# Expert rows transposed two blocks ahead, the gate's deviation by Newton steps on VectorE, and sorting by single spaced operations

## The chip, the cores and the metric

The kernel runs on one NeuronCore of a Trainium2 chip. Its engines work side by side, each through its own instructions in order: TensorE (PE, with its weight loads PEld), VectorE (DVE), ScalarE (ACT), GpSimd (POOL) and SyncE (SP), which here only issues DMAs. The metric is the device time of one execution in microseconds. The kernel before took 1323.85 us, the median of three runs (1323.38 to 1324.76).

## The reference

Two images of 256 channels and 56 x 56 points (N = 3136 tokens of C = 256) go through a linear non-local block, causal attention with 4 heads, and a mixture of 8 experts of which each token uses two. All is float32.

```python
x = _L0_conv_ref(x, ...)                       # non-local block, batch norm, + x, relu
t = _to_tokens(x)
t = t + _L1_attn_ref(_ln_t(t), W_attn, W_proj) # 4 heads, causal softmax
t = t + _L1_ffn_ref(_ln_t(t), gate_w, gate_b, W1, b1, W2, b2)
...
def _ln_t(v, eps=1e-5):
    m = jnp.mean(v, axis=-1, keepdims=True)
    s = jnp.var(v, axis=-1, keepdims=True)
    return (v - m) / jnp.sqrt(s + eps)
...
logits = xf @ gate_w + gate_b
probs = jax.nn.softmax(logits, axis=-1)
top2_vals, top2_idx = jax.lax.top_k(probs, 2)
# for each of the 8 experts, with its weight we per token:
h = jax.nn.gelu(xf @ w1 + bb1, approximate=False)
acc = acc + we[:, None] * (h @ w2 + bb2)
```

## The kernel before

A token tile is 128 tokens; an image has 25 (NCH), the last of 64 tokens. The kernel computes an expert's result only for the tokens that chose it: it sorts the two choices of every token into slots of DRAM tables `x_slots`, in blocks of 128 rows with one expert each, and works through 105 blocks (NBLK). The first 42 (FULL0) are filled by image 0 alone; the next 15 (up to MIXED = 57) may hold rows of both images; the rest belong to image 1.

**Stages.** The non-local block fills the first 96 us. Attention follows, image 0 up to about 495 us and image 1 up to 885 us. The experts run from 885 us to 1300 us, and a short tail writes the last outputs.

**Attention** (`attend`). Queries go in 7 blocks of 448; for each block and each pair of heads `hp` the key tiles are walked. A step computes scores on PE (L649), their Exp on ACT (L657), the causal mask on diagonal tiles (L659) and the running sum of the exponentials on DVE (L671), and three steps later (LAG) the values product on PE (L689). The result of a block lies in one PSUM buffer (`py`, bufs=1); ACT and DVE empty it at L699 and L700, and the next block's L689 waits for that. The division by the row sums makes a journey through DRAM: matmul with ones (L716), copy (L721), DMAs, reciprocal on DVE (L736), DMAs, product (L748). Each step of it is queued some steps after the one before.

**The order** is written by hand. Everything else is written as generators that yield between pieces; a `yield True` counts as a piece of work, a `yield False` says that nothing can be done now. In attention, `between` runs ahead of every score tile: in odd turns it pulls two pieces from `queue`, in even ones it issues steps of the projection to q, k and v (`project_qkv`). `pull` takes the next piece from the first generator in the queue that has one. The order in which pieces are issued is the order on each engine, and every engine keeps it.

For each image the queue has `tokens(b)`: `project_out` (attention's output projection for a tile, L598; sum and statistics on DVE, L603, L159, L160), then `dispatch(b)`, and for image 0 the loading of `w1s` (eight DMAs of 512 KB on SP), whose room is that of image 0's rows. So `dispatch(0)` and `project_out(1)` share the pulls during image 1's attention; `dispatch(1)` runs in the experts.

**`dispatch`** computes the gate and the sort: the deviation of each token (`inverse_deviation`: Sqrt on ACT, L166, reciprocal on DVE, L167), the gate's logits from sums that were made before (L955, L958), softmax (L961 to L967, with an Exp on ACT at L963), two maxima with their experts (L979 to L986), the ranks by matmuls with triangular and full ones (L1001, L1003), the slots (L1005 to L1077), the experts of the blocks (`first_blocks`, `last_blocks`, `one_hot`), and the scatter: for each tile the normalised rows (L1209, two buffers for image 0) and two indirect DMAs on POOL (L1217). Nearly all are small operations on DVE, of 128 x 200 or less. They are issued several at a time between yields (`small_piece`: three yields for image 0, one for image 1).

**`experts`**. Iteration n issues, in this order: the fetch of a group of three blocks from `x_slots` (`fetch`, six blocks ahead), the combination of a group's rows (`load`, two ahead; image 1's groups compute their places, L1281 to L1286, and mixed groups add rows, L1289), `hidden(n)` (16 matmuls at L1335, four Gelu on ACT at L1344), `inputs(n + 1)` (two transposes on PE at L1312, one copy to `xT` on ACT at L1316), `weights(n + 2)` (the expert's w1 copied by DVE, L1323), `outputs(n - 3)` (eight matmuls L1354, the bias on DVE, L1364, and the stores), and `between`: two or three pulls and one step of image 1's `last_blocks`. PSUM has two buffers each for transposes, hidden and output; `xT` has three, `w` two. The fetch of the first image 1 group comes at n = 36 and needs image 1's scatter.

Of the kernel before, what the change touches and what calls it, by code (L numbers as in the profile page):

```python
# [11 lines left out]
I32 = mybir.dt.int32  # L12
# [15 lines left out]
def conv_attn_moe_kernel(  # L28
# [133 lines left out]
    def inverse_deviation(b, n, m):  # L162
        r = ts[b][:, n : n + m, RSTD]

        d = ts[b][:, n : n + m, SLOT]
        nc.scalar.activation(d, r, AF.Sqrt, bias=eps5)  # L166
        nc.vector.reciprocal(r, d)  # L167
# [271 lines left out]
    def layer1(nm, general):  # L439

        with ExitStack() as whole:
# [147 lines left out]
            def project_out(b, qT, done):  # L589

                for first, m, k in pairs():
                    while done() < (first + m - 1) * P + k:
                        yield False
                    for n in range(first, first + m):
                        o = n * P
                        ps = bank(f"pp_{b}_{n}")
                        for c in range(NH):
                            nc.tensor.matmul(  # L598
                                ps[:k, : C + E], qT[:, c, o : o + k], wpr[:, c, :],
                                start=(c == 0), stop=(c == NH - 1),  # L600
                            )
                        t = ts[b][:k, n, : C + E]
                        nc.vector.tensor_tensor(t, t, ps[:k, : C + E], ALU.add)  # L603
                        stats(b, n, 1, k, bg, f"o{nm}{b}")
                        if b == 0:
                            nc.sync.dma_start(out=rest_d[:k, n], in_=t[:, :C])
                        yield True

                    for _ in range(2 if b == 0 else 0):
                        yield True  # L610
# [324 lines left out]
            def dispatch(b):  # L935
# [3 lines left out]
                inverse_deviation(b, 0, NCH)  # L939
                yield True  # L940

                def small_piece():

                    for _ in range(1 if b else 3):
                        yield True

                def small(name, last=E, dt=F32):
                    return g1.tile([P, NCH, last], dt, tag=name, name=f"{name}_{nm}{b}")
# [5 lines left out]
                red = small("red", 1)  # L954
                nc.vector.tensor_tensor(  # L955
                    pr, t[:, :, C : C + E], wide(t[:, :, RSTD : RSTD + 1]), ALU.mult
                )
                nc.vector.tensor_tensor(  # L958
                    pr, pr, gb.unsqueeze(1).to_broadcast([P, NCH, E]), ALU.add
                )  # L960
                nc.vector.tensor_reduce(red, pr, AX.X, ALU.max)  # L961
                nc.vector.tensor_tensor(pr, pr, wide(red), ALU.subtract)
                nc.scalar.activation(pr, pr, AF.Exp)  # L963
                yield from small_piece()
                nc.vector.tensor_reduce(red, pr, AX.X, ALU.add)
                nc.vector.reciprocal(red, red)
                nc.vector.tensor_tensor(pr, pr, wide(red), ALU.mult)  # L967
                yield from small_piece()


# [5 lines left out]
                for k in range(2):  # L976
                    top = wts[b][:, :, k : k + 1]
                    one = small(f"one{k}")
                    nc.vector.tensor_reduce(top, src, AX.X, ALU.max)  # L979
                    nc.vector.tensor_tensor(at, src, wide(top), ALU.is_equal)  # L980
                    nc.vector.tensor_tensor(at, at, ids, ALU.mult)
                    yield from small_piece()
                    nc.vector.tensor_reduce(red, at, AX.X, ALU.max)
                    nc.vector.tensor_tensor(one, at, wide(red), ALU.is_equal)
                    if k == 0:
                        nc.vector.scalar_tensor_tensor(left, one, -2.0, pr, ALU.mult, ALU.add)  # L986
                        src = left
                    picks.append(one)
                    yield from small_piece()
                both = small("both")  # L990
                nc.vector.tensor_tensor(both, picks[0], picks[1], ALU.add)
                if tail < P:
                    nc.vector.memset(both[tail:, NCH - 1], 0.0)
                flat = both.rearrange("p t e -> p (t e)")
                yield from small_piece()

                if b:
                    yield True
# [8 lines left out]
                )  # L1007
                tot = g1.tile([P, E, NCH], F32, tag="tot", name=f"tot_{nm}{b}")
                nc.vector.tensor_copy(tot, total[:, : NCH * E].rearrange("p (t e) -> p e t", e=E))
                yield from small_piece()  # L1010
# [22 lines left out]
                )  # L1033

                first = few("first")
                nc.vector.tensor_tensor(first, ends[:, :, NCH - 1], cnt, ALU.subtract)
                nc.vector.tensor_tensor(ends, ends, tot, ALU.subtract)
                slot = g1.tile([P, NCH, E], F32, tag="both", name=f"slot_{nm}{b}")
                nc.vector.tensor_tensor(slot, ranks, ends.rearrange("p e t -> p t e"), ALU.add)
                yield from small_piece()  # L1040
# [26 lines left out]
                nc.vector.tensor_tensor(part, slot, spread(lim), ALU.is_lt)  # L1067
                nc.vector.tensor_tensor(part, part, spread(low), ALU.mult)
                yield from small_piece()
                nc.vector.tensor_tensor(slot, slot, spread(base), ALU.add)  # L1070
                nc.vector.tensor_tensor(slot, slot, part, ALU.add)
                yield from small_piece()
                for k in range(2):
                    nc.vector.tensor_tensor(at, slot, picks[k], ALU.mult)
                    nc.vector.tensor_reduce(red, at, AX.X, ALU.add)
                    flat = red.rearrange("p t o -> p (t o)")
                    nc.vector.tensor_scalar(  # L1077
                        idxs[b][:, k, :], flat, -float(known[b][0] * P), None, ALU.add
                    )
                    if b and k == 0:  # L1080
                        nc.vector.tensor_scalar(t[:, :, SLOT], flat, 1.0, None, ALU.add)
                    yield from small_piece()

                def one_hot(eb, w):
# [5 lines left out]
                    for _ in range(1 if b else 3):  # L1090
                        yield True
# [7 lines left out]
                def first_blocks():  # L1099
# [7 lines left out]
                    )  # L1107
                    eb = g1.tile([P, MIXED], F32, tag="eb", name=f"eb_{nm}{b}")
                    nc.vector.tensor_reduce(eb, past, AX.X, ALU.add)
                    yield from small_piece()  # L1110
                    step = g1.tile([P, MIXED], F32, tag="step", name=f"step_{nm}{b}")
                    nc.vector.tensor_scalar(step, number[:, :MIXED], nfull, -float(E), ALU.is_ge, ALU.mult)
                    nc.vector.tensor_tensor(eb, eb, step, ALU.add)
                    nc.vector.tensor_scalar(step, number[:, :MIXED], nfull, 0.0, ALU.subtract, ALU.max)
# [89 lines left out]
                for n in range(NCH):  # L1204
# [11 lines left out]
                    for k in range(2):  # L1216
# [11 lines left out]
                        yield True  # L1228
# [4 lines left out]
            def experts(w1s, w2s, b2s, ex, es, ps6, between, need, written):  # L1233
# [156 lines left out]
                for n in range(-1, NBLK + LATE):  # L1390
                    while len(fetched) * GB <= min(n + 6, NBLK - 1):
                        fetched.append(fetch(len(fetched)))
                    while len(groups) * GB <= min(n + 2, NBLK - 1):
                        groups.append(load(len(groups), *fetched[len(groups)]))
# [4 lines left out]
                    if n + 1 < NBLK:  # L1399
                        xin[n + 1] = inputs(n + 1, groups[(n + 1) // GB])  # L1400
# [419 lines left out]
```

## Time and profile before

The profiled execution took 1325.2 us, 1323.5 us of it the span that the trace covers.

| what | value |
|---|---|
| median of the timed runs | 1323.85 us |
| profiled execution, its span | 1325.2 us, 1323.5 us |
| mean granted clock of PE | 0.993 |
| L671, sum of exponentials, DVE, 128x896 | 288 times, 1092 ns |
| L657, Exp of scores, ACT, 128x896 | 316 times, 918 ns |
| L598, output projection, PE, 128x264 | 192 matmuls, 403 ns |
| L1335, hidden, PE, 128x128 | 1680 matmuls, 276 ns |
| L1217, scatter, POOL | 100 times, 1153 ns |
| L963, Exp of the gate, ACT, 128x200 | 2 times, 370 ns |
| L166, Sqrt of the gate, ACT, 128x25 | 2 times, 338 ns |
| table loads of ACT | 9 times, 1283 ns |

A matmul in float32 counts as two instructions. Matmuls overlap, so their mean is longer than the time from one to the next. A line of the timeline has the start, the busy time (of all instructions that were merged into it, x16 for instance), engine, line, operation, output<-input and shape; behind it, in brackets, the time for which the engine stood idle before it, and what ended that.

### The profile page before, as it was taken

Reading aid. Unit: us, or ns where it says so; the run is one execution under the profiler, and the core shown is the slowest. Engines: PE = TensorE matmul, PEld = TensorE weight load, DVE = VectorE, ACT = ScalarE, POOL = GpSimd, SP = SyncE. Lnnn points to the kernel's source line nnn. Section 1 sums busy time; section 2 is a strip of 40 time slices with the busy share of each in tenths; the row PEclk is TensorE's granted clock in tenths of the full one; section 3 lists DMA queues with packets and bytes.
Section 4 is the critical chain, followed back from the end, with each engine's and each line's share of the span. In section 5 each row is a group of like instructions: output and inputs, shape, how many; then the busy total and the mean of one; then the engine's idle time right before and its main releaser. Section 6 shows DMA issues by size and latency. Waiting matters only on the chain.

```text
span 1323.5 us, 28216 instructions
## 1 busy us (share of the span) xinstructions
PE 1281.4 (97%) x10647; PEld 811.4 (61%) x10647; DVE 791.9 (60%) x1657; ACT 613.2 (46%) x1247; POOL 311.8 (24%) x300
## 2 busy tenths in 40 slices
PE   8999999999999999989999999998999999999994
PEld 7875444444444444434444444447999999999994
DVE  1582555757777654565958788765754344555552
ACT  0145554555555555455554456554333333344441
POOL 1113110000000111110004444000176012765541
PEclk9999999999999999999999999999999999999997
DMA  9993000000000000100001112441254333666642
GB/s 298 384 327 131 16 24 25 24 16 24 9 17 13 21 1 8 41 9 9 16 17 56 53 54 87 176 139 40 81 169 156 93 112 100 187 208 198 187 153 71
DMA packets 111048, 123.96 MB, mean 94 GB/s; under 512 B 20095, under 2 KB 100620, under 8 KB 110904
## 3 DMA queue, kind: packets, MB, share of 16 engines
q1 hardware_dynamic: 96664, 92.89, 22.8%
q0 software_dynamic: 10416, 26.00, 5.9%
q10 hardware_dynamic: 3824, 3.18, 0.8%
q8 instruction: 88, 1.44, 0.5%
q14 instruction: 56, 0.46, 0.1%
HBM read 63.04 MB, written 60.81 MB: 94 GB/s over the span
## 4 chain that ended last, share of the span: by engine, by line
PE 92%; DVE 2%; ACT 2%; DMA 1%; issue 1%; POOL 1%; SPq 0%; DVEq 0%; ACTq 0%; POOLq 0%
PE yp_f L689 21%; PE sc_f L649 19%; PE ht_f L1335 14%; PE yp_f L1354 13%; PE qk_f L535 6%; PE pp_f L598 4%; PE v_f L554 4%; PE cp L321 3%; PE gram L252 3%; PE tp_f L1312 2%; ACT st_f L657 1%; PE sp_f L716 1%; PE yo_f L1477 1%; DVE acc_f L671 1%; PE xp_f L514 1%
## 5 line engine op out<-in xcount | busy, mean ns | idle before, releaser
L657 ACT ACTIVATE st_f<-sc_f 128x896 f32<-128x896 f32 (+5 forms) x400 | 333.8, 838 | 293.8 <-PE sc_f L649 265.4
L671 DVE TENSOR_TENSOR acc_f<-acc_f,st_f 128x896 f32<-128x896 f32 (+5 forms) x372 | 366.5, 985 | 170.0 <-ACT st_f L657 163.1
L689 PE MATMUL yp_f<-st_f,v_f 64*64 64x448 f32 (+6 forms) x3184 | 342.0, 505 | 7.7 <-DVE qT_f L700 6.5
L649 PE MATMUL sc_f<-qT_f,kT_f 64*64 64x448 f32 (+6 forms) x3184 | 342.3, 501 | 0.0
L1344 ACT ACTIVATE g_f<-ht_f,b1b 128x128 f32<-128x128 f32 x420 | 120.1, 369 | 223.5 <-PE ht_f L1335 223.4
L1335 PE MATMUL ht_f<-xT_f,w_f 128*128 128x128 f32 x1680 | 205.8, 276 | 5.8 <-ACT xT_f L1316 5.8
L649 PEld LDWEIGHTS sc_f<-qT_f,kT_f 64*64 64x64 f32 x3184 | 117.6, 133 | 151.7 <-issue 137.5
L689 PEld LDWEIGHTS yp_f<-st_f,v_f 64*64 64x64 f32 x3184 | 111.7, 133 | 159.3 <-issue 132.1
L1335 PEld LDWEIGHTS ht_f<-xT_f,w_f 128*128 128x128 f32 x1680 | 201.6, 192 | 12.5 <-ACT xT_f L1316 7.7
L497 POOL TENSOR_SCALAR xn_f<-t 128x256 f32<-128x256 f32 (+1 forms) x50 | 67.1, 1351 | 549.6 <-issue 333.6
L1217 POOL DMA_INDIRECT x_slots<-xr_f,idx x100 | 115.3, 1153 | 214.9 <-DVE xr_f L1209 136.4
L1323 DVE COPY w_f<-w1s_f 128x1024 f32 x105 | 73.8, 703 | 59.8 <-PE ht_f L1335 58.5
L1371 POOL DMA_INDIRECT y_tokens<-ys_f,to_f x63 | 64.4, 1022 | 148.7 <-DVE ys_f L1364 138.9
L535 PE MATMUL qk_f<-px_f,wat 128*128 128x512 f32 (+1 forms) x224 | 92.4, 558 | 1.2 <-ACT px_f L520 1.2
L1364 DVE TENSOR_TENSOR ys_f<-yp_f,kT_f 128x128 f32<-128x128 f32 x105 | 30.5, 291 | 102.8 <-PE yp_f L1354 102.7
L659 DVE TENSOR_TENSOR st_f<-st_f,keep 128x256 f32<-128x256 f32 (+1 forms) x112 | 44.1, 394 | 66.2 <-ACT st_f L657 65.8
L535 PEld LDWEIGHTS qk_f<-px_f,wat 128*128 128x128 f32 x224 | 38.6, 190 | 54.2 <-issue 44.8
L1354 PE MATMUL yp_f<-px_f,g_f 128*128 x210 | 62.7, 381 | 0.0
L1354 PE MATMUL yp_f<-v_f,g_f 128*128 x210 | 62.5, 379 | 0.0
L1354 PE MATMUL yp_f<-w2s_f,g_f 128*128 x210 | 62.5, 379 | 0.0
L1354 PE MATMUL yp_f<-kT_f,g_f 128*128 x210 | 62.5, 379 | 0.0
L1427 POOL DMA_INDIRECT y_f<-y_slots,idx x50 | 55.4, 1108 | 16.3 <-issue 14.0
(249 smaller groups left out, 1174.4 us busy)
## 6 DMA issues: line engine op xcount, KB each, us to landing
x_slots<-fill SPq DMA_DIRECT2D x1, 8127.0 KB
xb_f<-x_slots SPq DMA_DIRECT2D x63, 129.0 KB
x_slots<-fill SPq DMA_DIRECT2D x1, 7296.0 KB
y_slots<-ys_f SPq DMA_DIRECT2D x57, 128.0 KB
kept<-t SPq DMA_DIRECT2D x2, 3200.0 KB
x<-in_x_dram SPq DMA_DIRECT2D x14, 448.0 KB
xr<-in_x_rows_dram SPq DMA_DIRECT2D x12, 512.0 KB
out_dram<-ot_f SPq DMA_DIRECT2D x24, 256.0 KB
```

The source lines that it names most:

```text
L497: nc.gpsimd.tensor_scalar(xn[:k, a], ts[b][:k, n + a, :C], ts[b][:k, n + a, MEAN : MEAN + 1], ts[b][:k, n + a, RSTD : RSTD + 1], ALU.subtr ...
L535: nc.tensor.matmul(ps[:, :w], wat[:, c, d0 : d0 + P], xT[:, c, :w], start=(c == 0), stop=(c == NH - 1),)
L649: nc.tensor.matmul(ps[h : h + HS, a, c0:W], kT[hp][rows, j * P + h : j * P + h + HS], qT[rows, hp, q0 + c0 : q0 + W], start=True, stop=True,)
L657: nc.scalar.activation(st[:k, :, c0:], ps[:k, :, c0:W], AF.Exp, scale=SCALE)
L671: nc.vector.tensor_tensor(acc[:k, :, c0:], acc[:k, :, c0:], st[:k, :, c0:], ALU.add)
L689: nc.tensor.matmul(yp[a * HS : (a + 1) * HS, h // HS, c0:W], v[hp][h : h + HS, j, a, :HS], st[h : h + HS, a, c0:], start=first, stop=bool( ...
L1217: s = nc.gpsimd.indirect_dma_start(out=xds[b], out_offset=bass.IndirectOffsetOnAxis(ap=idxs[b][:kk, k, n : n + 1], axis=0), in_=xr[:kk], i ...
L1323: nc.vector.tensor_copy(w, w1s[:, :, bass.ds(e, 1), :].rearrange("p c e h -> p c (e h)"))
L1335: nc.tensor.matmul(ht[:, k, :], w[:, c, k * P : (k + 1) * P], xT[:, c, :], start=(c == 0), stop=(c == NH - 1),)
L1344: nc.scalar.activation(g[:, k, :], ht[:, k, :], AF.Gelu, bias=b1bs[b][:, k, i : i + 1])
L1354: nc.tensor.matmul(yp[:, :C], g[:, k, :], w2s[k][:, bass.ds(e, 1), :].rearrange("p e d -> p (e d)"), start=(k == 0), stop=(k == KH - 1),)
L1371: s = nc.gpsimd.indirect_dma_start(out=y_tokens, out_offset=bass.IndirectOffsetOnAxis(ap=to[:, n % GB : n % GB + 1], axis=0), in_=ys, in_o ...
```

## The change

- **`project_out`**: image 1's two tiles of a pair are issued together and followed by two yields; before, there was a yield after each tile. Image 0 keeps its order.
- **`dispatch`, deviation**: in place of Sqrt on ACT and a reciprocal, four Newton steps for the inverse square root on DVE, with a start value from integer operations: 3 operations, then 4 x 4, all of 128 x 25. `inverse_deviation` remains for the non-local block and for the branch that isn't taken here.
- **`dispatch`, spacing**: a new generator `op` yields once or twice, in turn, after nearly every operation for image 0, and not at all for image 1; `small_piece` yields once for image 1 and not at all for image 0. The Exp of the gate gets yields ahead of it in both.
- **`dispatch`, scatter**: for image 0 one yield per tile instead of two, so that both indirect DMAs of a tile are issued together.
- **`experts`**: `inputs` runs two blocks ahead instead of one, and `load` three instead of two.

```diff
                         stats(b, n, 1, k, bg, f"o{nm}{b}")
                         if b == 0:
                             nc.sync.dma_start(out=rest_d[:k, n], in_=t[:, :C])
-                        yield True
-
-                    for _ in range(2 if b == 0 else 0):
+                            yield True
+
+                    for _ in range(2):
                         yield True
...
-                inverse_deviation(b, 0, NCH)
-                yield True
+                ops = [0]
 
                 def small_piece():
 
-                    for _ in range(1 if b else 3):
+                    if b:
+                        yield True
+
+                def op():
+
+                    ops[0] += 1
+                    for _ in range(0 if b else 1 + ops[0] % 2):
                         yield True
...
+                var = t[:, :, RSTD]
+                x, y, z = (
+                    small(k, 1).rearrange("p t o -> p (t o)") for k in ("newton_x", "newton_y", "red")
+                )
+                nc.vector.tensor_scalar(x, var, 1e-5, None, ALU.add)
+                nc.vector.tensor_scalar(
+                    y.bitcast(I32), x.bitcast(I32), 1, None, ALU.arith_shift_right
+                )
+                nc.vector.tensor_scalar(
+                    y.bitcast(I32), y.bitcast(I32), -1.0, float(0x5F3759DF), ALU.mult, ALU.add
+                )
+                yield from small_piece()
+                for i in range(4):
+                    to = var if i == 3 else y
+                    nc.vector.tensor_tensor(z, y, y, ALU.mult)
+                    nc.vector.tensor_tensor(z, z, x, ALU.mult)
+                    nc.vector.tensor_scalar(z, z, -0.5, 1.5, ALU.mult, ALU.add)
+                    nc.vector.tensor_tensor(to, y, z, ALU.mult)
+                    yield from op()
+                    yield from small_piece()
...
                 nc.vector.tensor_tensor(pr, pr, wide(red), ALU.subtract)
+                yield from op()
+                yield from small_piece()
                 nc.scalar.activation(pr, pr, AF.Exp)
                 yield from small_piece()
+                yield from op()
                 nc.vector.tensor_reduce(red, pr, AX.X, ALU.add)
+                yield from op()
...
-                        yield True
+                        if b or k:
+                            yield True
                     if b == 0:
                         yield False
...
-                    while len(groups) * GB <= min(n + 2, NBLK - 1):
+                    while len(groups) * GB <= min(n + 3, NBLK - 1):
                         groups.append(load(len(groups), *fetched[len(groups)]))
...
-                    if n + 1 < NBLK:
-                        xin[n + 1] = inputs(n + 1, groups[(n + 1) // GB])
+                    for m in (n + 1, n + 2):
+                        if m < NBLK and m > n + 1 - (n < 0):
+                            xin[m] = inputs(m, groups[m // GB])
```

Behind almost every other operation of `dispatch` stands the same `yield from op()`.

## The prediction, made before the changed kernel had run

> **What bounds the kernel now.** First the page: PE is busy 1281.4 us of a span of 1323.5 us, and it carries the chain of waits.
>
> ```profile
> PE 1281.4 (97%) x10647; PEld 811.4 (61%) x10647; DVE 791.9 (60%) x1657; ACT 613.2 (46%) x1247; POOL 311.8 (24%) x300
> ...
> PE 92%; DVE 2%; ACT 2%; DMA 1%; issue 1%; POOL 1%; SPq 0%; DVEq 0%; ACTq 0%; POOLq 0%
> ```
>
> The change adds and removes no matmul. It can win only where PE stands still, where its clock is lowered, or where the order of matmuls costs something. So the second view is the timeline of PE alone, read for the brackets (idle time before an instruction, and its releaser). Of the 42 us idle, 6 are at the start, 8 in the tail; the ones that the change reaches are these:
>
> ```profile
> 572.70 0.59 PE L716 MATMUL sp_f<-acc_f,ones 128*32 128x224 f32 x8 [2.52 <-ACT v_f L563]
> ...
> 592.36 0.98 PE L689 MATMUL yp_f<-st_f,v_f 64*64 64x448 f32 x8 [1.72 <-DVE qT_f L700]
> ...
> 602.17 0.56 PE L689 MATMUL yp_f<-st_f,v_f 64*64 64x192 f32 x8 [0.61 <-DVE st_f L659]
> ...
> 643.50 1.73 PE L689 MATMUL yp_f<-st_f,v_f 64*64 64x448 f32 x16 [0.79 <-DVE qT_f L700]
> ...
> 890.10 2.05 PE L1335 MATMUL ht_f<-xT_f,w_f 128*128 128x128 f32 x16 [1.28 <-ACT xT_f L1316]
> ...
> 918.43 2.05 PE L1335 MATMUL ht_f<-xT_f,w_f 128*128 128x128 f32 x16 [0.41 <-ACT xT_f L1316]
> ...
> 923.79 2.05 PE L1335 MATMUL ht_f<-xT_f,w_f 128*128 128x128 f32 x16 [1.36 <-ACT xT_f L1316]
> ```
>
> The stall of 890.10 comes twice more, 1.28 us each, at 893.64 and 897.19: blocks 1, 2 and 3 of the experts. From 925 to 1297 us PE shows no gap; a block there takes 3.73 us (16 matmuls of hidden 1.78, two transposes 0.22, eight of the output 1.73).
>
> Third, stages of 4 us around the first stall; columns are stretch, length, busy time of PE, PEld, DVE, ACT and POOL, granted clock, DMA share, GB/s.
>
> ```profile
> 568.00:572.00 4.00, 2.17 (x16) 1.18 (x8) 2.93 (x6) 0.86 (x3) 1.66 (x2) 1.00 0.00 0
> 572.00:576.00 4.00, 3.31 (x32) 1.42 (x36) 1.63 (x2) 1.97 (x6) 0.76 (x1) 0.74 0.00 1
> 576.00:580.00 4.00, 4.00 (x28) 2.03 (x24) 3.20 (x6) 1.63 (x5) 0.00 (x0) 0.83 0.02 1
> ```
>
> After the gap the clock is 0.74 and 0.83: 4 x 0.26 + 4 x 0.17 = 1.72 us of PE time lost besides the 2.52.
>
> **Gate of image 0 (561 to 660 us).** The timeline of ACT tells why PE stopped:
>
> ```profile
> 561.93 1.28 ACT L166 ACT_TABLE_LOAD   x1
> ...
> 564.00 1.28 ACT L657 ACT_TABLE_LOAD   x1
> ...
> 571.14 0.37 ACT L963 ACTIVATE lg_f<-lg_f 128x200 f32<-128x200 f32 x1 [3.13 <-DVE lg_f L962]
> ```
>
> Sqrt costs two table loads and 0.34 us; then the Exp of the gate, queued in ACT ahead of the scores' Exp and the copies of v, waits 3.13 us for a clump of four DVE operations (L955 to L962). Newton removes the loads and keeps Exp's table in place; Exp moves behind the third score tile of the next block row. Gain 2.52 + 1.72 = **4.2 us**. The price is 19 operations of 128x25 on DVE. No row has exactly these; the nearest, L1077 (128x25), takes 180 ns, and small ones follow each other every 0.2 us: 3.8 us, less the reciprocal's 0.32. Seven stand just ahead of the evacuation L700 that began at 564.02; 1.4 us fit there, since PE computes q and k until 565.41 and needs L700's result at 566.2. The rest is spread over DVE's idle time (55% busy from 550 to 575 us, 71% from 575 to 600). Cost on the path 0; uncovered it would be 3.5.
>
> What is late next: Exp still waits for L962, now issued behind L700 and one sum of image 1's second score row. ACT finishes the scores before it at 590.9 in today's times, L962 can end near 592.9: ACT stands 2 us, but the score tile behind it is needed by PE only near 595.8. Ends: 0 (covered) and 2 idle us with another 1.7 of clock; I take **+0.5**, nearer to cover.
>
> Single operations instead of clumps: ahead of L700 at 591.70 stand three (L983, L984, L986; 1.1 us), in the changed order one (0.36): -0.75. At 602.17 two become one: -0.5 of 0.61. At 643.50 five (1.2 us) become L984 ahead and L991, L993 behind: -0.35. Against it four of 0.2 us (L1114 to L1088) now stand ahead of the L700 of 705 us, where one of 0.41 stood: +0.3. Sum **-1.3**.
>
> **Projection of image 1 in pairs.** With one yield per pair (L607, L609), tiles 0 to 17 of L598 are issued as nine pairs, not eighteen singles. The timeline of PE prices that. A single (711.35 us) lasts 1.08 to its successor, and the neighbours of other shape lose 0.12 ahead and 0.06 behind against their usual 0.75: 1.26. A pair (image 0's at 545.38) takes 1.97 + 0.12 + 0.06 = 2.15. Nine times 2 x 1.26 - 2.15 = 0.37 is **-3.3 us**, all on PE. DVE gets the two tiles' sum and statistics as a clump, 2 x (0.42 + 0.43 + 0.18) = 2.06 us, and the second PSUM buffer is asked for sooner; PE itself spends 1.97 us there, and scores run three tiles ahead of values. Ends 0 and 1.43 per pair (the third rival); I take **+0.5** in all.
>
> **Scatter.** Per tile of image 0 one yield goes, so a pull of two brings one tile and one turn of the projection. POOL then issues two indirect DMAs of 1.28 us per turn of two score tiles (over 3 us), and the row buffer is reused two turns later: covered; uncovered, 2.6 us per tile. The queue of w1 (SP, eight of 512 KB) is issued a little earlier among the w2 loads, hidden behind attention in both. 0 us.
>
> **Start of the experts.** With transposes two blocks ahead the three waits of 1.28 us, 3.84 together, go. But w of block 3 (L1323) stands behind the reciprocal L736 in DVE's queue, and that waits for the row sums' journey through HBM:
>
> ```profile
> 895.88 0.20 DVE L736 RECIPROCAL back_f<-sums 128x7 f32<-128x7 f32 x1 [6.55 <-DMA sums<-sums]
> 896.07 0.69 DVE L1323 COPY w_f<-w1s_f 128x1024 f32 x1
> ```
>
> The order on DVE is the same after the change. Block 3 starts at 897.19 now and can't before 896.8; so the three short waits become one of about 4.3 us. The second transpose and its copy (0.39, L1316) now stand ahead of L716's sums and L721, so the journey ends 0.4 us later, and projection tile 21 waits for it (L748; PE has 0.36 us in hand). [...] The row at 568 us: 2.52 us idle, then 1.72 us of clock lost; three gaps of 1.28 with 2 us of work between lost nothing (875 to 900 us at 1.00). [...] Of this 0.8 hides in the wait for tile 21: loss 0.4 (no dip) to 1.3; I take **+0.9**. Without the journey the gain would be 3.8.
>
> **Gate of image 1 (911 to 924 us).** Of four table loads two go; Exp and Gelu's return stay, 1.28 + 0.37 + 1.28 = 2.93 us on ACT, with two blocks of 3.73 us until that xT is needed. Both stalls go: **-1.8**. Two Newton steps per block are 8 x 0.2 = 1.6 us beside 1.26 (w copy, two sums): 2.9 of 3.73 on DVE, covered. The scatter (POOL, 50 x 1.38 = 69 us) starts three blocks later and ends near 1032 instead of 1022; the first fetch of those rows was issued on SP at 1034.4 and moved its data until 1042 (DMA share by the microsecond). It may go 2 us later; its group is combined one block sooner, near 1044 instead of 1048, and PE wants it near 1049: 0, and uncovered 2.
>
> **Sum.** -4.2 + 0.5 - 1.3 - 3.3 + 0.5 + 0.9 - 1.8 = **-8.7 us**. The profiled execution took 1325.2 us, 1.7 outside its span: 1316.5. The median of the timed runs is 1323.85, so **1315.2** there. The tail (5.92 us for y_tokens at 1312.91) is untouched. What a measurement can tell from no change is 0.2%, 2.65 us.
>
> **Rivals.**
> - The start of the experts does win: -3.8 in place of +0.9, 1310.5. For it: three visible stalls. Against: the two DVE lines above. 0.07.
> - The stall of 572 us only moves to the new place of Exp: 2 us idle and 1.7 of clock, less the 0.5 taken, 1318.4. For it: ACT's 3.13 us wait was for DVE, not for tables alone. Against: PE's slack there. Or attention is so tight on DVE that pairs win nothing: 1315.2 + 3.3 = 1318.5. Together 0.22.
> - **Slower:** DVE becomes the bound from 700 to 790 us, where it is 74 to 84% busy. Each pair holds DVE for a second tile and a scatter row, 1.02 + 0.41 = 1.43 us, and PE waits for L659, L700 or the PSUM buffer. Nine times is 12.9: 1328.1. It decides from 0.97 us per pair, where the 8.7 are used up. For it: L700 has one PSUM buffer and no slack. Against: PE is full there now, and the pair occupies PE as long as DVE. 0.05.
> - My forecast, 0.66.
>
> Its own range is 1312.5 to 1318; with the second rival and part of the first, 1311.5 to 1320.5. Faster by over 0.2% (below 1321.2): 0.89; within 0.06; slower 0.05.
>
> **What would show it.** No Sqrt load at 562; clock 1.00 from 572 to 580; L598 in runs of x8; one gap of about 4 us before block 3, a clock below 1 after it, L748 unchanged near 900; no wait for xT at 910 to 930; blocks still 3.73 us. It is wrong if PE idles before L689 from 690 to 790, or if block 3 starts by 893.

## The result, and the profile after

The changed kernel took **1319.67 us** (median of four runs, 1318.96 to 1320.43), the kernel before in the same set 1323.62 us (1323.25 to 1324.76). The ratio is 0.9966, with a 95% interval of 0.9951 to 0.9981: faster, by 4.0 us where 8.7 were forecast. The profiled span is 1318.6 us, 4.9 less than that of the profile before. In that profile the first score tile starts 0.39 us later than before (the first input DMAs; over all profiles of this study it starts between 109.28 and 110.48 us), so differences below are counted from there or between two events of the same profile.

The page of the changed kernel, busy time by engine and the chain that ended last:

```profile
PE 1277.5 (97%) x10647; PEld 814.1 (62%) x10647; DVE 793.3 (60%) x1693; ACT 606.9 (46%) x1241; POOL 311.6 (24%) x300
...
PE 90%; DVE 3%; DMA 3%; ACT 1%; issue 1%; POOL 0%; SPq 0%; ACTq 0%; DVEq 0%; POOLq 0%
```

PE has the same 10647 matmuls and is busy 3.9 us less. The mean granted clock is 0.993 in both profiles, so this is how the matmuls follow one another, not work. DVE has 36 instructions more and only 1.4 us of busy time. In the chain DMA has gone from 1% to 3%.

The idle times of PE, from its timeline (in brackets the idle time before the instruction, and what ended it):

```profile
588.37 0.98 PE L689 MATMUL yp_f<-st_f,v_f 64*64 64x448 f32 x8 [1.48 <-DVE qT_f L700]
...
652.98 0.66 PE L689 MATMUL yp_f<-st_f,v_f 64*64 64x256 f32 x8 [1.13 <-DVE st_f L659]
...
698.62 1.73 PE L689 MATMUL yp_f<-st_f,v_f 64*64 64x448 f32 x16 [0.84 <-DVE qT_f L700]
...
705.02 1.16 PE L598 MATMUL pp_f<-wpr,qT_f 128*128 128x264 f32 x4 [0.30 <-DVE b1b L1154]
...
778.38 1.73 PE L689 MATMUL yp_f<-st_f,v_f 64*64 64x448 f32 x16 [1.41 <-DVE qT_f L700]
...
888.74 0.41 PE L1375 MATMUL tp_f<-ident,xb_f 128*128 128x128 f32 x2 [1.67 <-DMA xb_f<-x_slots]
...
893.84 3.24 PE L1398 MATMUL ht_f<-xT_f,w_f 128*128 128x128 f32 x16 [2.69 <-DVE w_f L1386]
```

The 2.52 us at 572 us are gone, and so are the three waits of 1.28 us for xT and those at 918 and 924 us. New are the lines at 653, 698, 705, 778, 889 and 894 us. (L1375, L1379, L1386 and L1398 are the L1312, L1316, L1323 and L1335 of before; L598 to L748 keep their numbers.) Two of the new waits are read on DVE's timeline:

```profile
776.38 0.41 DVE L1271 TENSOR_SCALAR xr_f<-t 128x256 f32<-128x256 f32 x1 [1.67 <-DMA x_slots<-xr_f,idx]
776.71 1.08 DVE L671 TENSOR_TENSOR acc_f<-acc_f,st_f 128x896 f32<-128x896 f32 x1
777.71 0.61 DVE L700 TENSOR_TENSOR qT_f<-qT_f,yp_f 128x448 f32<-128x448 f32 x1
...
892.81 0.20 DVE L736 RECIPROCAL back_f<-sums 128x7 f32<-128x7 f32 x1 [7.02 <-DMA sums<-sums]
893.00 0.69 DVE L1386 COPY w_f<-w1s_f 128x1024 f32 x1
...
899.09 0.63 DVE L748 TENSOR_TENSOR qT_f<-qT_f,rb_f 128x448 f32<-128x448 f32 x1 [5.40 <-DMA rb_f<-inverses]
```

At 776 us a scatter row of image 0 waits for its buffer, behind it stands the L700 that PE's next values product needs: that is the 1.41 us. At 893 us the weights of block 3 stand behind the reciprocal, as the forecast had it. Of the merged gap a part lies one block earlier (1.67 us, the fetch of the second group's rows), the rest before block 3, and behind it the clock is lowered. Windows of 4 us (the number after POOL is the granted clock):

```profile
892.00:896.00 4.00, 2.16 (x12) 2.19 (x13) 0.88 (x2) 0.37 (x2) 1.03 (x2) 0.80 0.02 2
896.00:900.00 4.00, 4.00 (x20) 3.63 (x19) 0.91 (x2) 1.40 (x5) 0.59 (x2) 0.77 0.18 57
```

That is 4 x 0.20 + 4 x 0.23 = 1.72 us; block 3 takes 3.24 us instead of 2.05. From 556 to 596 us the clock is 1.00 now.

### The profile page after: what moved, and what is told of

Its sections match the earlier page's. It is cut to its first block, busy times and chain, and to the rows that moved or that the text cites. A ratio compares the mean times of both kernels' runs of the same rounds, so it can differ in the third digit from the quotient of the medians.

```text
span 1318.6 us, 28242 instructions
## 1 busy us (share of the span) xinstructions
PE 1277.5 (97%) x10647; PEld 814.1 (62%) x10647; DVE 793.3 (60%) x1693; ACT 606.9 (46%) x1241; POOL 311.6 (24%) x300
## 4 chain that ended last, share of the span: by engine, by line
PE 90%; DVE 3%; DMA 3%; ACT 1%; issue 1%; POOL 0%; SPq 0%; ACTq 0%; DVEq 0%; POOLq 0%
PE yp_f L689 20%; PE sc_f L649 18%; PE ht_f L1398 14%; PE yp_f L1417 13%; PE qk_f L535 7%; PE v_f L554 4%; PE pp_f L598 4%; PE cp L321 3%; PE gram L252 2%; PE tp_f L1375 2%; DVE acc_f L671 1%; ACT st_f L657 1%; PE sp_f L716 1%; PE yo_f L1541 1%; PE xp_f L514 1%
## 5 line engine op out<-in xcount | busy, mean ns | idle before, releaser
L689 PE MATMUL yp_f<-st_f,v_f 64*64 64x448 f32 (+6 forms) x3184 | 340.5, 503 | 10.1 <-DVE qT_f L700 8.3
L689 PEld LDWEIGHTS yp_f<-st_f,v_f 64*64 64x64 f32 x3184 | 112.2, 133 | 162.9 <-issue 131.8
L1398 PE MATMUL ht_f<-xT_f,w_f 128*128 128x128 f32 x1680 | 206.6, 276 | 2.7 <-DVE w_f L1386 2.7
L1398 PEld LDWEIGHTS ht_f<-xT_f,w_f 128*128 128x128 f32 x1680 | 203.0, 193 | 7.9 <-issue 3.3
L1386 DVE COPY w_f<-w1s_f 128x1024 f32 x105 | 73.5, 701 | 60.4 <-PE ht_f L1398 60.2
L1491 POOL DMA_INDIRECT y_f<-y_slots,idx x50 | 55.9, 1118 | 16.3 <-issue 13.7
```

What stands on the lines that cost most here:

```text
L689: nc.tensor.matmul(yp[a * HS : (a + 1) * HS, h // HS, c0:W], v[hp][h : h + HS, j, a, :HS], st[h : h + HS, a, c0:], start=first, stop=bool( ...
L1386: nc.vector.tensor_copy(w, w1s[:, :, bass.ds(e, 1), :].rearrange("p c e h -> p c (e h)"))
L1398: nc.tensor.matmul(ht[:, k, :], w[:, c, k * P : (k + 1) * P], xT[:, c, :], start=(c == 0), stop=(c == NH - 1),)
```

## The experiments

All stretches in this table come from the profiles: A from the row sums' matmul at 549 us (L716, the 17th) to the end of the last attention matmul; B from there to block 4's hidden product; C from there to block 20's. "idle" and "clock" are the parts of A that lie in brackets and in the lowered clock. "journey" is the time from the end of attention to L748, the last step of the row sums' way through DRAM.

| kernel | A, us | idle, clock in A | B, us | journey, us | C, us | ratio to before (95%) |
|---|---|---|---|---|---|---|
| before | 336.37 | 5.87, 1.71 | 18.30 | 16.93 | 66.06 | 1 |
| changed | 332.45 | 6.21, 0 | 19.33 | 17.36 | 63.40 | 0.9966 (0.9951, 0.9981) |
| e1 Newton only | 333.36 | 4.43, 0 | 19.28 | 17.90 | 65.18 | 0.9987 (0.9979, 0.9994) |
| e2 one ahead | 332.07 | 5.85, 0 | 17.65 | 16.27 | 65.78 | 0.9974 (0.9965, 0.9982) |
| e3 singles | 332.48 | 4.06, 0 | 19.94 | 17.69 | 63.40 | 0.9964 (0.9951, 0.9977) |
| e4 scatter by row | 330.44 | 3.84, 0 | 21.55 | 18.13 | 63.39 | 0.9952 (0.9939, 0.9965) |
| e5 spread | 329.98 | 3.73, 0 | 18.65 | 16.36 | 63.39 | 0.9943 (0.9929, 0.9957) |
| e6 gap filled | 332.47 | 6.24, 0 | 19.26 | 16.92 | 63.39 | 0.9963 (0.9949, 0.9977) |
| e7 late chain | 332.42 | 6.19, 0 | 13.17 | 17.46 | 65.18 | 0.9922 (0.9908, 0.9935) |
| e8 one, then two | 332.13 | 5.88, 0 | 18.13 | 16.76 | 63.48 | 0.9948 (0.9935, 0.9962) |

In e7 two projection turns have moved from B to C, so there B + C counts: 78.35 against 82.73. The wait at 588 us varies with a DMA of the row sums (1.02 to 1.48 us in profiles with the same code up to there), so half a microsecond of A is chance. The journey is spread over 16.3 to 18.1 us, and B follows it: in the kernel before, e1, e2 and e8, and in e9 and e12 below, block 4 starts 1.4 us behind L748. In the changed kernel it is 2.0. So of the 1.0 us by which B grew, 0.4 is a longer journey and 0.6 the merged gap with its lowered clock; e1, with no merged gap and a full clock, has nearly the same B (19.28), with a journey of 17.90 us.

**e1: Newton steps alone, on the kernel before.** The four operations ahead of Exp stay one clump.

```diff
-                inverse_deviation(b, 0, NCH)
-                yield True
...
+                nc.vector.tensor_scalar(x, var, 1e-5, None, ALU.add)
...
+                for i in range(4):
...
+                    nc.vector.tensor_tensor(to, y, z, ALU.mult)
+                    yield True
```

> The kernel before, with only the reciprocal deviation of the gate by Newton steps (19 operations on VectorE with four places to interleave); the four operations L955 to L962 stay one clump ahead of Exp, sorting, projection, scatter and transposes stay as before. Theory A (the Exp that waits for a clump, queued in ACT ahead of the scores, makes the stall of image 0's gate; tables only add to it): Exp now stands ahead of the fourth whole score tile, whose evacuation began at 574.2 us in the changed kernel, while DVE ends the last Newton step and the clump near 577.0 us; TensorE idles 2 to 3 us near 576 with a clock below 0.9 behind it. The gain is then image 1's gate alone, about 2 us: near 1321.6. Theory B (the two table loads make the stall): no idle over 1 us between 565 and 585 us and clock 1.00; gain 4.2 + 2 = 6.2: near 1317.4.

The timeline of PE (L1351 and L1332 are the hidden product and the copy to xT in this kernel's numbering):

```profile
577.18 0.98 PE L649 MATMUL sc_f<-qT_f,kT_f 64*64 64x448 f32 x8 [0.46 <-ACT st_f L657]
...
588.09 0.98 PE L689 MATMUL yp_f<-st_f,v_f 64*64 64x448 f32 x8 [1.72 <-DVE qT_f L700]
...
900.01 0.71 PE L598 MATMUL pp_f<-wpr,qT_f 128*128 128x264 f32 x2 [1.31 <-DVE qT_f L748]
...
927.79 2.05 PE L1351 MATMUL ht_f<-xT_f,w_f 128*128 128x128 f32 x16 [1.45 <-ACT xT_f L1332]
```

And ACT's, where Exp waits for the clump:

```profile
575.96 0.37 ACT L979 ACTIVATE lg_f<-lg_f 128x200 f32<-128x200 f32 x1 [3.72 <-DVE lg_f L978]
```

For image 0 the numbers are those of theory B: where 2 to 3 us were expected, 0.46 are left. The cause is open, though. Exp waits longer than before (3.72 us against 3.13), but the four new yields have also moved it: the copies of v that PE waited for at 572 us now stand ahead of it. So an Exp behind a clump need not stop PE; whether the loads that went or the new place removed the stall, this run doesn't separate. A falls by 3.01 us, not by 4.2, since 1.1 us of idle comes up in other places, most of it the 0.46, and 1.01 instead of 0.61 at 598 us. But the last line of PE's timeline contradicts theory B for image 1: one block still waits 1.45 us for xT at that gate, though Sqrt's loads are gone. C falls by 0.88 only.

**e2: transposes one block ahead again.**

```diff
-                    while len(groups) * GB <= min(n + 3, NBLK - 1):
+                    while len(groups) * GB <= min(n + 2, NBLK - 1):
...
-                    for m in (n + 1, n + 2):
-                        if m < NBLK and m > n + 1 - (n < 0):
-                            xin[m] = inputs(m, groups[m // GB])
+                    if n + 1 < NBLK:
+                        xin[n + 1] = inputs(n + 1, groups[(n + 1) // GB])
```

> The changed kernel with expert rows transposed one block ahead again (three waits of about 1.3 us for xT instead of one merged gap). Theory A (merged gap costs a throttled clock, transposes two ahead win nothing at image 1's gate because that stall was table loads): clock 1.00 from 885 to 900 us, block 4 starts about 19.3 us after the end of attention instead of 20.3, no wait for xT over 0.5 us from 905 to 930: about 1.0 faster than the changed kernel, near 1318.7. Theory B (the early transposes are what removed the stalls at image 1's gate): waits of 1 to 2 us for xT come back between 905 and 930 us, and the time is 1320 to 1321.

Half of each theory. B is 1.7 us shorter, with clock 1.00. But 1.1 of it is a shorter journey (16.27 us against 17.36); 0.6 is what the merged gap and its clock cost. And C is 2.4 us longer: PE waits 2.04 us for xT at 929 us. ACT's timeline there tells why:

```profile
923.18 1.28 ACT L995 ACT_TABLE_LOAD   x1
926.30 0.37 ACT L995 ACTIVATE lg_f<-lg_f 128x200 f32<-128x200 f32 x1 [1.84 <-DVE lg_f L992]
926.69 1.28 ACT L1407 ACT_TABLE_LOAD   x1
...
929.00 0.39 ACT L1379 COPY xT_f<-tp_f 128x256 f32<-128x256 f32 x1
```

Exp's load, its wait for the last logits operation on DVE, Exp and Gelu's load hold ACT from 923.2 to 928.0 us, and the copy of the transposed rows stands behind them. The changed kernel has the same sequence three microseconds later, but there that xT is needed a block later.

**e12: transposes two ahead alone, on the kernel before** (the same edit in the other direction). It was run once, in a later set on another chip, of which more under e10; up to block 20 its trace shows none of the stretches described there.

> The kernel before with only the transposes two blocks ahead; Sqrt with its tables, sorting, projection and scatter as before. Theory A (at image 1's gate it is the early transposes that hide ACT's work, not the two table loads that go): from block 4 to block 20 of the experts 63.4 to 64 us, as in the changed kernel (63.40), instead of 66.06 before, though Sqrt's loads stay. Theory B (ACT's four loads, Sqrt and Exp with their waits are longer than two blocks): 64.5 to 66. Both: attention as before, block 4 about 1 us later behind its end than the 18.3 us of before (merged gap).

ACT's timeline there:

```profile
912.08 1.28 ACT L166 ACT_TABLE_LOAD   x1
...
917.91 1.28 ACT L963 ACT_TABLE_LOAD   x1
...
922.85 0.39 ACT L1316 COPY xT_f<-tp_f 128x256 f32<-128x256 f32 x1
```

Theory A: C is 63.76 us, with all four table loads still there (the other two, back to Gelu, come at 915 and 921 us), and PE does not wait for xT. B is 19.37, with a journey of 18.00 us. So the gain at image 1's gate belongs to the early transposes, and the Newton steps add 0.4.

**e8: one ahead up to block 3, two ahead from there.**

```diff
+                made = set()
...
-                        if m < NBLK and m > n + 1 - (n < 0):
+                        if m < NBLK and m not in made and m <= n + 1 + (n > 2):
+                            made.add(m)
```

> The changed kernel with expert rows transposed one block ahead up to block 3 and two ahead from there. Theory A (the two gains are independent: one ahead spares the merged gap and its clock, as the run with one ahead showed by 2.0 us at block 4; two ahead spares the wait of 2.04 us for xT at image 1's gate): both are kept, about 2 faster than the changed kernel, near 1317.7. Theory B (block 4's start is set by the journey of the last row sums, whose length varies by 1 to 2 us from run to run whatever the transposes do): block 4 starts 19.5 to 20.5 us behind the end of attention, time 1319 to 1320.

Theory A by its result: B 18.13, C 63.48, together 1.1 us less than in the changed kernel, whose interval it still overlaps. But theory B names what sets block 4's start: it is 1.4 us behind L748 here as in e2. Of the 1.2 us gained in B, 0.6 is a journey shorter than the changed kernel's, and 0.6 the merged gap and its clock.

**e6 and e9: the gap before block 3 filled with matmuls** that nothing reads, 22 and then 12 of them.

```diff
+                    if n == 3:
+                        fill = bank("fill")
+                        for _ in range(FILL):
+                            nc.tensor.matmul(fill[:, :P], ident, ident, start=True, stop=True)
```

> The changed kernel with 22 extra matmuls of 128x128 (about 2.4 us) on TensorE ahead of block 3 of the experts, into a spare bank that nothing reads: they fill the gap in which block 3 waits for its weights. Theory A (the lowered clock behind the gap costs): clock 1.00 from 892 to 900 us, block 3 takes 2.05 us instead of 3.24, and block 4 starts 1 to 1.7 us earlier behind the end of attention than the 20.3 us of the changed kernel's profile: near 1318.5. Theory B (the journey of the last row sums through HBM is what block 4 waits for; gap and lowered clock lie in its shadow): clock 1.00 and block 3 short, but the projection's tile still starts when L748 lets it, block 4 at 20.3 less 0.3 at the most: within 0.4 of the changed kernel's 1319.7.

The 22 took 4.91 us, twice what I had reckoned (a float32 matmul counts as two instructions; the 12 of e9 below are x24), and held block 3 back to 895.44 us. The clock was 1.00 throughout, and B stayed at 19.26: the filling cost what the clock gave. That decides nothing between the theories; hence e9.

> As the run with the filled gap, with 12 extra matmuls of 128x128: the 22 took 4.91 us, 0.22 each, and so held block 3 back to 895.44 us. Twelve take 2.7 us, which is the gap. Theory A (the lowered clock costs in full): block 3 begins near 893.4 us and takes 2.05 us, block 4 starts 1.7 us earlier behind the end of attention than in the changed kernel (19.3 us, counted from the end of the last attention matmul): 17.6. Theory B (the last row sums' journey is next in line): the projection's second tile waits for L748, and block 4 starts at 18.4 to 19.1 us.

The timeline of PE in e9 (its attention ended at 885.91 us; the last two lines are for further below):

```profile
894.68 2.84 PE L1464 MATMUL fill_f<-ident 128*128 128x128 f32 x24
897.61 2.02 PE L1399 MATMUL ht_f<-xT_f,w_f 128*128 128x128 f32 x16
...
903.23 0.71 PE L598 MATMUL pp_f<-wpr,qT_f 128*128 128x264 f32 x2 [0.31 <-DVE qT_f L748]
...
994.16 0.27 PE L1399 MATMUL ht_f<-xT_f,w_f 128*128 128x128 f32 x1 [0.94 <-issue]
994.88 0.27 PE L1399 MATMUL ht_f<-xT_f,w_f 128*128 128x128 f32 x1 [0.44 <-issue]
```

Block 3 takes 2.02 us, and B is 18.01, between both expectations: the lowered clock costs up to 1.3 us here, and then L748 is what PE waits for (0.31 us). With the journey of the changed kernel's profile, 0.7 us longer, about half of the 1.3 would be left: again 0.6 us.

**e7: the row sums' last steps over more turns.** The reciprocal L736 goes one block later, behind the weights of block 3, L748 another one, and the last projections two.

```diff
+                    turns = 0
                     while finished[B - 1][NH - 1] < N:
...
                         due(clock[0])
-                        yield True
-                        yield True
+                        turns += 1
+                        for _ in range(4 if turns < 3 else 2):
+                            yield True
```

> The changed kernel with the last row sums' steps spread over more turns of the experts' loop: the reciprocal L736 is issued one block later, behind the weights' copy of block 3, L748 one block later again, and the last projections stand two blocks later. Theory A (the journey costs only because in-order queues make TensorE wait for it): no gap before block 3, clock 1.00, no wait for L748, four to five blocks beside the journey; by the trace 4 us gained at block 9 against the changed kernel. Image 1's sorting and scatter move two blocks (7.5 us) later, less the gain; its rows are needed near 1049 us, which costs nothing if the slack is over 3.5 us: near 1315.7. Theory B (image 1's rows then come late): TensorE idles 1 to 4 us between 1035 and 1060 us, and the time is 1317 to 1319.5.

DVE's timeline:

```profile
886.39 0.70 DVE L1386 COPY w_f<-w1s_f 128x1024 f32 x1 [1.31 <-PE ht_f L1398]
...
892.06 0.20 DVE L736 RECIPROCAL back_f<-sums 128x7 f32<-128x7 f32 x1 [4.98 <-DMA sums<-sums]
...
898.47 0.63 DVE L748 TENSOR_TENSOR qT_f<-qT_f,rb_f 128x448 f32<-128x448 f32 x1 [3.30 <-DMA rb_f<-inverses]
```

The weights of block 3 are copied at 886.4 instead of 893.0 us. The journey is no shorter (L748 is 17.46 us behind the end of attention), but PE does blocks 3, 4 and 5 meanwhile and has no wait from block 3 on. Theory A: 4.4 us by the trace, ratio 0.9922, whose interval lies below that of the changed kernel. No wait for image 1's rows appears; from block 20 to block 60 it gives back 0.1 us against the changed kernel.

**e3: image 1's projection a tile at a time**, and **e4: the old yield after each scatter**.

```diff
# e3, in project_out
-                            yield True
-
-                    for _ in range(2):
+                        yield True
+
+                    for _ in range(2 if b == 0 else 0):
                         yield True
# e4, in dispatch
-                        if b or k:
-                            yield True
+                        yield True
```

> The changed kernel with image 1's projection a tile at a time again. Forecast's arithmetic (0.37 us per pair, nine pairs): 3.3 slower, near 1323.0. Theory from the two traces (a pair's second tile waits for PSUM, and a clump on DVE gives part of it back): about 1.5 slower, near 1321.2, and the idle of 0.30 us at 705 us goes. Pairs worth nothing: 1319.7.

> The changed kernel with the old yield after each of the two scatters of a tile of image 0. Theory A (the scatter a tile at a time overruns POOL; the row buffer xr comes free late and L700 queues behind it): the 1.41 us idle of TensorE near 778 us goes and nothing replaces it, about 1.4 faster than the changed kernel, near 1318.3. Theory B (the projection's pairs cause it, or the later scatter delays w1 and the stall moves): within 0.4 of 1319.7.

e3: A is the same, 332.48 against 332.45. Pairs are worth nothing in sum, but not because nothing happens: without idle and clock, A is 328.42 us with singles and 326.24 with pairs, so the order of matmuls saves 2.2 us (0.24 a pair, where 0.37 was forecast). The idle time is 4.06 with singles and 6.21 with pairs. From the first score tile to the row sums at 775 us pairs lead by 1.6 us; then comes the wait of 778 us, which only the changed kernel's combination shows. Neither e3 (scatter by tile, singles) nor e4 (scatter by row, pairs) has it.

e4: theory A for attention. The idles at 705 and 778 us are gone, A falls by 2.0 (0.46 of it the varying wait). But B grows by 2.2 (0.8 of it a longer journey), and by block 20 nothing is won in the trace (0.2 us lost). After a wait of 1.29 us for rows and one of 3.90 before block 3 the clock is lowered twice as long. Windows of e4:

```profile
888.00:892.00 4.00, 0.29 (x3) 0.05 (x1) 0.84 (x2) 1.40 (x5) 0.92 (x2) 0.94 0.02 3
892.00:896.00 4.00, 3.82 (x18) 3.85 (x19) 0.04 (x1) 0.02 (x1) 1.28 (x3) 0.50 0.16 44
896.00:900.00 4.00, 4.00 (x15) 3.35 (x14) 2.42 (x5) 1.38 (x5) 0.00 (x0) 0.71 0.07 18
```

4 x (0.06 + 0.50 + 0.29) = 3.40 us. The timed ratio (0.9952) does look better than the changed kernel's, but the intervals overlap.

**e5: more places to interleave** in the clumps that the change had left.

```diff
                     nc.vector.tensor_copy(numi, cnt)
+                    yield True
...
                 nc.vector.tensor_copy(num, numi)
+                for _ in range(0 if b else 2):
+                    yield True
...
                 nc.vector.tensor_tensor(first, ends[:, :, NCH - 1], cnt, ALU.subtract)
+                if b == 0:
+                    yield True
...
                     nc.vector.tensor_tensor(early, eb, step, ALU.add)
+                    yield True
+                    yield True
```

> The changed kernel with five more places to interleave: the counts and ends of image 0 (L1064 to L1086, eight operations in one piece ahead of a diagonal mask) in four pieces, and two turns between the last two block operations (L1176, L1177) and the copy of the experts' numbers (L1145, L1147). Theory A (these clumps alone make the idles of 1.13 us at 653 us and 0.85 us at 698 us): both go, 2.0 faster than the changed kernel by the trace up to image 1's row sums at 735 us, near 1317.7. Theory B (DVE is the bound of these stretches, so that the same work shows up as another wait): idle of TensorE from 640 to 740 us within 0.5 of the 2.8 us that the changed kernel shows, time within 0.5 of it.

Theory A, and a little more: the 1.13 at 653 us is gone, 0.84 has become 0.59, and the scatter, which now starts at 711.7 us instead of 704.9, no longer holds up L700 at 778 us; its rows wait 0.8 us each at 786 and 789 us, where PE loses nothing. Against that, 0.80 instead of 0.30 us wait for the bank at the first pair. A falls by 2.5, idle by the same (0.46 of it the varying wait). The interval of the ratio still overlaps that of the changed kernel.

**e10: e5 and e7 together; e11: the same with singles.**

> The changed kernel with both edits that won: more places to interleave in image 0's counts and block operations, and the last row sums' steps spread over more turns of the experts' loop. If the two gains are independent, they add: by the traces 3.2 and 4.4 us on the changed kernel's 1319.7, near 1312.1. Rival: with attention ending 3 us earlier, the last fetch of expert rows or image 1's rows come late, and 1 to 3 us of it are lost again: 1313 to 1315.

> The run with both edits, but image 1's projection a tile at a time. In the changed kernel pairs saved 2.2 us of order on TensorE and cost 2.15 us of idle (1.41 at 778 us, 0.30 at 705 us, the rest in the first waits); with the clumps spread the idle of 1.41 is gone. Theory A (pairs are worth their order once the stall is gone): singles 1.5 to 2.2 slower than with pairs. Theory B (a pair's clump on DVE costs as much as it saves wherever it falls): within 0.5 of the run with pairs.

These two, e9 and e12 ran in a set, on another chip, in which the kernel before itself took 1361.07 us. The traces show what differs: mainly from about 790 us on there are stretches, such as the last two lines of e9 above, in which PE gets its matmuls singly, one every 0.71 us, with the idle time put down to issue; why, the traces do not show. So neither expectation in microseconds can be judged. The ratios in that set are 0.9853 (0.9825 to 0.9881) for e10 and 0.9876 (0.9851 to 0.9902) for e11, and do not separate them. What lies ahead of these stretches can be read: up to the row sums at 773 us e10 follows e5 within 0.7 us, and pairs are 1.5 us ahead of singles. Whether that lasts to the end when the wait at 778 us is gone, and whether the gains of e5 and e7 add in full, stays open. The best version with a ratio from outside this set is e7.

## Why the prediction was right in sign and too large

The forecast was faster by 8.7 us. Up to block 20 the profile of the changed kernel gained 5.6 (420.73 - 415.18 from the row sums at 549 us); the span 4.9, since the first score tile starts 0.4 us later and the rest behind block 20 takes 0.3 longer. Term by term:

| step | forecast | measured | shown by |
|---|---|---|---|
| image 0's gate, stall and clock | -4.2 | -3.0 | e1 against before, A |
| Exp's new place, single operations, scatter by tile | +0.5 - 1.3 + 0 | -0.9 | e3 against e1, A |
| pairs of image 1's projection | -3.3 + 0.5 | 0.0 | changed against e3, A |
| start of the experts | +0.9 | +1.0 | B |
| image 1's gate | -1.8 | -2.7 | C |
| sum | -8.7 | -5.6 | |

**Image 0's gate.** The stall went as forecast, by the removed loads and the moved Exp together (e1 does not part them); the term was mis-sized by 1.2. Filling a stall of 2.52 us gave 1.4 us of it, since other waits came up behind. The clock term did come back (1.71), but it was luck that it could: e12 has the same stall of 2.52 us with the same sequence on ACT, and its clock was not lowered at all.

**Spacing.** The sum agrees, but not term by term. Of the 0.9 us only 0.4 is idle time. The stall that was feared at Exp's new place (+0.5) did not come: PE shows no gap from 549 to 588 us. Against that, the forecast named four operations ahead of the L700 of 705 us at +0.3 (it stalls 0.84 at 698 us, where before it was under 0.15) and missed the eight in one piece ahead of the mask at 653 us (1.13). e5 shows that these are the price of clumps left over, not a bound of DVE.

**Pairs and scatter: here the forecast failed.** Two of its steps read: "Ends 0 and 1.43 per pair (the third rival); I take +0.5 in all", and of the scatter "covered; uncovered, 2.6 us per tile. ... 0 us". Each is nearly true alone (e4 and e3). Together they are not: a turn now brings a second tile's 1.02 us and a scatter row of 0.41 us to DVE, and two indirect DMAs to POOL. Around 770 us three of these took 1.8 to 2.1 us each where 1.0 is usual; the rows of two tiles were made at 769.92 and 772.28 us, and the third tile's waited until 776.38 for one of the two buffers, with L700 behind it. Why those three took longer stays open. The 0.30 at 705 us is the PSUM buffer that was named. So the order on PE won 2.2, and idle time took 2.15 back: the second rival's "pairs win nothing", by way of the slower rival's place, though at a sixth of its price. The sign that was named in advance for it, PE idle ahead of L689 between 690 and 790 us, is there.

**Start of the experts.** Right in place and mechanism: block 3 at 893.84, behind the weights that stand behind the reciprocal; 1.72 us lost to the clock; L748 at 899.09. That the size agreed is in part luck: 0.4 of the 1.0 us is a longer journey, as forecast, but that journey varies by more than this from profile to profile, and only 0.6 of the 1.72 us of clock reached block 4. The forecast's 1.7 us of clock was the loss behind the stall of 2.52 us, carried over to a gap of about 4.3 us; that was an estimate of mine. The runs do not agree on how much idle time costs clock, but they do on the size of a loss. In rows of 4 us 1.72 us are lost behind 2.52 us of idle (before), 1.72 behind 1.67 and 2.69 with a block's work between (changed), 1.72 behind 2.37 (e12, 892 to 896 us at 0.57), 3.40 with 1.29 and 3.90 (e4, 0.24 of it in a row in which PE is busy for 0.29 us); 0.95 and 2.70 in e5, with a block's work between, cost 1.7. Narrower rows, first of the kernel before, then of the changed one, show where the clock is lowered:

```profile
572.90:573.90 1.00, 1.00 (x16) 0.36 (x12) 1.00 (x2) 0.58 (x2) 0.00 (x0) 1.00 0.00 0
573.95:577.36 3.41, 3.41 (x24) 1.33 (x20) 1.10 (x3) 0.70 (x1) 0.00 (x0) 0.50 0.02 2
577.36:578.36 1.00, 1.00 (x10) 0.47 (x3) 0.93 (x4) 0.30 (x1) 0.00 (x0) 1.00 0.00 0
...
893.40:894.40 1.00, 0.56 (x5) 0.59 (x6) 0.29 (x1) 0.00 (x0) 0.47 (x1) 1.00 0.00 0
894.40:897.81 3.41, 3.41 (x18) 3.31 (x17) 0.00 (x0) 0.69 (x3) 1.06 (x2) 0.50 0.20 60
897.85:898.85 1.00, 1.00 (x6) 0.87 (x5) 0.00 (x0) 0.67 (x3) 0.00 (x0) 1.00 0.06 20
```

In both PE works at 1.00 again for a while behind the gap (1.24 us from 572.70, 0.56 us from 893.84), then at 0.50 for 3.41 us, which is 1.71 us lost; the 3.40 us of e4 are twice that. What sets the start and the length of such a stretch was not shown.

**Image 1's gate.** Right in sign, wrong in cause. The step was: "Of four table loads two go ... Both stalls go". e1 and e2 show that the stall stays at 1.45 and 2.04 us without Sqrt's loads, e12 that it goes though they are there. The early transposes do it. They were charged with the loss at the start and given none of this gain.

## What to carry to other kernels

When two edits each put something into the same turn of an in-order queue, price the turn with both in it: buffers that last for one may not be enough for the two (here two row buffers, and 1.41 us at 778 us). A long wait at the head of an in-order queue (DVE's 7.02 us ahead of L736) costs what stands behind it; put what the starved engine needs ahead of it, as e7 did (block 3's weights at 886.4 instead of 893.0 us). A stall that is filled need not come back in full (1.4 of 2.52 us at image 0's gate, 0.6 of 1.72 us of clock at the start of the experts): look for the wait that ends next, L748's in the second case. And before crediting a gain to the operation that was removed, ask which other edit gives the waiter more slack.

## What the runs showed of the hardware that was not expected

The clock lost behind a gap is not a function of the gap's length alone: behind the same 2.52 us of idle 1.72 us were lost in the kernel before and none in e12. The windows of e12 around the same stall as in the kernel before, where they read 1.00, 0.74 and 0.83:

```profile
568.00:572.00 4.00, 2.32 (x20) 1.19 (x11) 2.93 (x6) 0.86 (x3) 1.52 (x2) 1.00 0.00 0
572.00:576.00 4.00, 3.16 (x40) 1.28 (x40) 1.89 (x3) 2.32 (x6) 0.90 (x1) 1.00 0.00 1
```

PE is busy 2.32 and 3.16 us in them, against 2.17 and 3.31 before: the same idle time, and no loss. Why, the traces do not show; e12 ran on another chip than e1 to e8. On the chip of those the mean clock of the kernel before also varied, from 0.992 to 0.995 over 26 runs; one loss of 1.71 us is 0.0013 of the span. A gain that rests on the clock should be given as 0 or 1.7 us with a chance, not as its mean.

The journey of the last row sums (L716 to L736, through DRAM and back) took 9.7 us in e2, 10.3 in the changed kernel and 11.2 in e4, with the same DMAs. And two streams of the same matmuls differed by 2.2 us in their order alone, with no bracket to show it (e3 and the changed kernel): nine times, a second tile of L598 stands behind the first instead of between score matmuls of another shape.
